# The second stage of a graph network: from generators with due times to a planner of operations for all engines

## The chip, the cores and the metric

The kernel runs on one core of one Trainium2 chip. The metric is the device time of one execution in microseconds (us). A core has a matrix engine (TensorE, PE in the profile), a vector engine (VectorE, DVE), an activation engine (ScalarE, ACT), a small general engine (GpSimd, POOL), and a queue engine (SyncE, SP) from which most transfers (DMAs) are issued. Each runs its own list of instructions in the order in which the program holds them, and waits on semaphores for the others. All data are float32.

## The reference, cut to what matters

`x` is 128 graphs of 64 nodes with 256 features: 8192 rows. Each layer is `x = layernorm(x + f(x))`.

```python
# layer 0: A = adj * adj            h = relu(A (x W1)); h = relu(A (h W2)); f = A (h W3)
# layer 1: U = eigenvectors of a normalised Laplacian of adj
#          f = U (relu((U.T x) W1 + b1) W2 + b2)
# layer 2: h = relu(adj (x Wg0 + bg0)); h = relu(adj (h Wg1 + bg1))
#          for p in 1..4: an LSTM over windows of p nodes; its last state
#          overwrites node p-1 of every window; f = h
# layer 3: h = x W + b_lin; s = (h h.T) * adj, zeros to -1e16; f = softmax(s) h + b
```

## The kernel before

The 8192 rows stand in the on-chip memory as one tile `X` of 64 tiles of 128 rows (a tile holds two graphs). Four tiles make a group, so there are 16 groups.

**Stage one** is layer 0 of all groups, with the eigenvector computation of layer 1 threaded between its matmuls on the DVE. It ends about 860 us into the run and isn't touched by the change, but for the order in which it takes the groups and where their rows lie.

**Stage two** is layers 1 to 3, group by group. A group is a Python generator (`group`, calling `layer1`, `layer2`, `lstm`, `layer3`) that issues instructions and yields the time at which it can go on. Up to `WAYS = 3` groups are open. The PE's order is written by hand: `now` is a clock that advances by an account of each matmul, and at each turn the loop at the end takes, of the groups whose yielded time has come, the oldest one (or, when no group is left to open, the one that is least far on). The yielded times are coarse constants, for example:

```python
MOVE, MIXED, LIN, CONV, NORM, SOFT = 1.2, 1.2, 1.5, 1.8, 5.2, 5.2
CELL = {256: 3.8, 168: 2.2, 128: 1.9}
...
ready.append(now[0] + NORM + more + (0.8 if ready else 0.0))
```

DVE, ACT and POOL aren't ordered by hand in stage two: a scheduler of the framework orders what was issued, with two copies put ahead (`high_priority`). Scratch tiles come from rotating pools: `pw` with 5 buffers, `pv` with 4, `pg` with 3 each for gates, cell and state, and `psb`, the 8 banks of PSUM.

The chains that cross engines, by their lines in the profile:

- layer 1 (`layer1`): `ps<-u,X`, copy to `w`, `ps<-bw,w`, add of the bias on DVE (L971), relu on ACT (L725), `ps<-ut,v`, copy (L979), `ps<-bw,v`, add to `X` (L986), and the norm: `bn_stats` and `bn_aggr` (L551, L552) on DVE, two operations on POOL (L553, L554), and `X<-X,ln_mv,ln_rs` (L564) on DVE. Layer 2 then begins with `ps<-adT,X`.
- LSTM step: per half `h` and gate four matmuls (two with `wih` on the inputs, two with `whh` on the state `hs`; each shows as two records), then `tanh` on ACT (L1030), the cell update on DVE (L1034, L1036, L1038), `tanh` of the cell (L1039), and the new `hs` (L1041), which the `whh` matmuls of the next step read. The last state of a window is written back into `hT`, a tile `w` (L1051).
- layer 3: transposes of `X` (L926), two copies (L1120, L1124), `ps<-w,dw`, identity with bias (L1130), scores (L1146), softmax on DVE and ACT (L1150 to L1159), transposes of `att`, copy `eT` (L1166), `ps<-w,v`, add to `X` (L1176), norm, output.

The last two groups (`ENDING`) take layer 3 in two halves of two tiles and do the last step of the norm on ACT (L562).

Of the kernel before, what the change touches and what calls it, by code (L numbers as in the profile page):

```python
# [1 line left out]

# [8 lines left out]
F32 = mybir.dt.float32  # L11
# [4 lines left out]
N = 64  # L16
# [24 lines left out]
class Timed:  # L41
# [6 lines left out]
    def __getattr__(self, name):  # L48
        def give(out, *args, **kw):
            self.free[0] = max(self.free[0], self.until[0]) + self.least + 0.0009 * max(0, np.prod(out.shape[1:]) - 64)  # L50
            return getattr(self.engine, name)(out, *args, **kw)  # L51

        return give

# [484 lines left out]
LEAD = 10  # L539
# [57 lines left out]
def kernel(  # L597
# [51 lines left out]
    X = keep.tile([P, NT, D], F32, name="X")  # L649
# [4 lines left out]
    nc.scalar.dma_start(X[:, 2:4, :], x_t[:, 2:4, :])  # L654
    for t in range(2):
        nc.sync.dma_start(X[:, t, :], x_t[:, t, :])
# [6 lines left out]
    for t in range(4, NT, 2):  # L663
        nc.sync.dma_start(X[:, t:t + 2, :], x_t[:, t:t + 2, :])
# [79 lines left out]
    def layer0(g):  # L744
        xs = X[:, 4 * g:4 * g + 4, :]
# [108 lines left out]
        for t in (2, 0):  # L854
            p = tl(psa, [P, 2, D], "ps", bufs=6)
            mm(p, sqT2, s3[:, t:t + 2, :])
            yield now[0]
            x2 = xs[:, t:t + 2, :]
            VL.tensor_add(x2, p, x2)
            norms.extend(scalar_norm(tc, small, x2, half, spare))  # L860

# [45 lines left out]
    pg = ctx.enter_context(tc.tile_pool(name="pg", bufs=WAYS, reuse_waits="tile"))  # L907
    pw = ctx.enter_context(tc.tile_pool(name="pw", bufs=5, reuse_waits="tile"))
    pv = ctx.enter_context(tc.tile_pool(name="pv", bufs=4, reuse_waits="tile"))
    psb = ctx.enter_context(tc.tile_pool(name="psb", bufs=8, space=bass.MemoryType.PSUM, reuse_waits="tile"))  # L910
# [10 lines left out]
    now[0] = due[0] = 0.0  # L921
    MOVE, MIXED, LIN, CONV, NORM, SOFT = 1.2, 1.2, 1.5, 1.8, 5.2, 5.2
    CELL = {256: 3.8, 168: 2.2, 128: 1.9}

    def turn(out, in_):
        PE.transpose(out, in_, ident)  # L926
        now[0] += 0.11

    def work():
        return tl(pw, [P, 1024], "w")  # L930

    def work2():
        return tl(pv, [P, 512], "v")

    spare[0] = lambda: work2()[:, :D]

    def ps4(shape=(P, 512)):
        return tl(psb, list(shape), "ps")
# [4 lines left out]
    def mixed(src, rhs, ready):  # L943
# [3 lines left out]
        for t in range(4):  # L947
            if t % 2 == 0:
                yield ready[t // 2]
            for c in range(2):  # L950
                mm(ps[c][:, t * P:(t + 1) * P], src[:, t, c * P:(c + 1) * P], rhs)
        with tc.high_priority(offset=1500):
            V.tensor_copy(dst[:, 0, :], ps[0])
        S.copy(dst[:, 1, :], ps[1])
        yield now[0] + MIXED
        return dst

    def norm(xs, t, ready, more=0.0, scalar=False):
        rows_norm(tc, small, xs[:, t:t + 2, :], half, scalar)
        ready.append(now[0] + NORM + more + (0.8 if ready else 0.0))  # L960

    def layer1(xs, ready):
        a = yield from mixed(xs, u2, ready)
        for t in range(0, 4, 2):
            V.tensor_add(xs[:, t:t + 2, :], xs[:, t:t + 2, :], ub2.unsqueeze(1).to_broadcast([P, 2, D]))
        h = as3(work2(), 4)
        for t in range(0, 4, 2):
# [5 lines left out]
            yield now[0]  # L973
        yield now[0] + LIN
        z = work2()
        p = ps4((P, 4, P))
        for t in range(4):
            mm(p[:, t, :], h[:, t, :], ut2)
        S.copy(as3(z, 4), p)  # L979
        yield now[0] + MOVE  # L980
        ready = []
        for t in range(0, 4, 2):
            p = ps4((P, 2, D))
            for j in range(2):
                mm(p[:, j, :], z[:, (t + j) * P:(t + j + 1) * P], bw2)
            V.tensor_add(xs[:, t:t + 2, :], p, xs[:, t:t + 2, :])  # L986
            norm(xs, t, ready, 2.0)
            yield now[0]
        return ready

    def lstm(hT, p, first, nw):
# [6 lines left out]
        for t in range(p):  # L998
# [4 lines left out]
            G = tl(pg, [P, 2048], "gates")[:, :2 * len(names) * n].rearrange("p (q h n) -> p q h n", h=2, n=n)  # L1003
            gate = {q: G[:, i] for i, q in enumerate(names)}
            units = [(h, q) for h in range(2) for q in names]

            ahead = {}
            early = units[:2] if t else []
            for h, q in early:
                m = slice(("ifgo".index(q) * 2 + h) * P, ("ifgo".index(q) * 2 + h + 1) * P)  # L1010
                ahead[h, q] = pp = ps4()[:, :n]
                for k in range(2):
                    mm(pp, wi[:, k, m], xt[k], k == 0, False)
            if t:
                yield ready
            if p > 1 and not t:
                c = tl(pg, [P, 512], "c")[:, :2 * n].rearrange("p (h n) -> p h n", h=2)
            new = None if last else tl(pg, [P, 512], "hs")[:, :2 * n].rearrange("p (h n) -> p h n", h=2)
            for h, q in units:
                j = 2 * "ifgo".index(q) + h  # L1020
                m = slice(j * P, (j + 1) * P)
                pp = ahead.get((h, q))
                if pp is None:
                    pp = ps4()[:, :n]
                    for k in range(2):
                        mm(pp, wi[:, k, m], xt[k], k == 0, k == 1 and not t)
                if t:
                    for k in range(2):
                        mm(pp, wh[:, k, m], hs[:, k, :], False, k == 1)
                S.activation(gate[q][:, h, :], pp, AF.Tanh, bias=bias[:, j:j + 1], scale=0.5 if q == "g" else 0.25)  # L1030
                if q == "g":
                    to = gate["g"][:, h, :] if t or p == 1 else c[:, h, :]
                    if t:
                        V.scalar_tensor_tensor(c[:, h, :], gate["f"][:, h, :], 1.0, c[:, h, :], op0=ALU.add,  # L1034
                                               op1=ALU.mult)
                    V.scalar_tensor_tensor(to, gate["i"][:, h, :], 1.0, gate["g"][:, h, :], op0=ALU.add, op1=ALU.mult)  # L1036
                    if t:
                        V.scalar_tensor_tensor(c[:, h, :], c[:, h, :], 0.5, to, op0=ALU.mult, op1=ALU.add)  # L1038
                    S.activation(gate["i"][:, h, :], c[:, h, :] if p > 1 else to, AF.Tanh, scale=0.5)  # L1039
                if q == "o" and not last:  # L1040
                    V.scalar_tensor_tensor(new[:, h, :], gate["o"][:, h, :], 1.0, gate["i"][:, h, :], op0=ALU.add,  # L1041
                                           op1=ALU.mult)
                if q == "o":
                    if h == 0:
                        yield now[0]
                elif h == 1 or len(units) == 8:
                    yield now[0]
# [7 lines left out]
            ready = now[0] + CELL[n]  # L1055
            hs = new
        return ready

    def layer2(xs, g, ready):
        a = yield from mixed(xs, adT2, ready)  # L1060
        g1 = as3(work(), 4)
        ready = []
        for t in range(0, 4, 2):
            p = ps4((P, 2, D))
            for j in range(2):
                run(p[:, j, :], [(a[:, k, (t + j) * P:(t + j + 1) * P], cw0[:, k, :]) for k in range(2)])
            V.tensor_add(g1[:, t:t + 2, :], p, wide["c_b0"].unsqueeze(1).to_broadcast([P, 2, D]))
            relu(g1[:, t:t + 2, :], g1[:, t:t + 2, :])
            ready.append(now[0] + CONV)
            yield now[0]  # L1070
        a = yield from mixed(g1, adT2, ready)
        hT = tl(pw, [P, 1024], "w").rearrange("p (k n b) -> p k n b", k=2, b=8)
        for c in range(2):
            p = ps4((P, 4, P))
            run(p, [(cw1[:, k, c * P:(c + 1) * P], a[:, k, :]) for k in range(2)])
            h = work2()
            V.scalar_tensor_tensor(as3(h, 4), rs_row.unsqueeze(1).to_broadcast([P, 4, P]), cb1[:, c:c + 1], p,
                                   op0=ALU.mult, op1=ALU.add)
            S.activation(hT[:, c, :, :].rearrange("p n b -> p b n"), as3(h, 8), AF.Relu, scale=2.0)
            yield now[0]  # L1080
        ready = now[0] + CONV
        for p, first, nw in ((1, 0, 32), (1, 32, 32), (2, 0, 32), (3, 0, 21), (4, 0, 16)):
            if first == 0:
                yield ready
            ready = yield from lstm(hT, p, first, nw)
        hb = as3(work(), 2)
        V.tensor_copy(as3(hb[:, 0, :], 8), hT[:, 0, :, :].rearrange("p n b -> p b n"))
        S.copy(as3(hb[:, 1, :], 8), hT[:, 1, :, :].rearrange("p n b -> p b n"))
        yield ready + 1.6
        ready = []  # L1090
        for t in range(0, 4, 2):
            p = ps4((P, 2, D))
# [169 lines left out]
```

## Time and profile before

| | |
|---|---|
| time, three runs | 2534.43, 2536.52, 2536.97 us; median 2536.52 |
| span of the profiled execution | 2539.1 us |
| PE busy | 2494.8 us (98%) |
| weight loads busy | 2196.2 us (86%) |
| DVE, ACT, POOL busy | 1407.8, 1090.6, 134.2 us |
| mean granted PE clock | 0.993 |
| DMA | 32.09 MB, mean 13 GB/s |

The PE is busy nearly throughout, so the chain of waits that ended last is 91% PE. A busy PE isn't a PE at its peak, since matmuls are pipelined and their ends are modelled. What a change of order can move is therefore in the rest: the idle time of the PE by place, the stretches in which its granted clock is below 1, and the distance between the starts of its matmuls. A window of the trace gives, for a stretch of time, how long each engine was busy in it, with the number of its instructions, the granted clock, the share of the DMA engines and their rate.

### The profile page before, as it was taken

Reading aid. Unit: us, or ns where it says so; the run is one execution under the profiler, and the core shown is the slowest. Engines: PE = TensorE matmul, PEld = TensorE weight load, DVE = VectorE, ACT = ScalarE, POOL = GpSimd, SP = SyncE. Lnnn points to the kernel's source line nnn. Section 1 sums busy time; section 2 is a strip of 40 time slices with the busy share of each in tenths; the row PEclk is TensorE's granted clock in tenths of the full one; section 3 lists DMA queues with packets and bytes.
Section 4 is the critical chain, followed back from the end, with each engine's and each line's share of the span. In section 5 each row is a group of like instructions: output and inputs, shape, how many; then the busy total and the mean of one; then the engine's idle time right before and its main releaser. Section 6 shows DMA issues by size and latency. Waiting matters only on the chain.

```text
span 2539.1 us, 39015 instructions
## 1 busy us (share of the span) xinstructions
PE 2494.8 (98%) x15020; PEld 2196.2 (86%) x15020; DVE 1407.8 (55%) x4996; ACT 1090.6 (43%) x2706; POOL 134.2 (5%) x316
## 2 busy tenths in 40 slices
PE   9999999999999999999999999999999999999997
PEld 7788887888878889998989889898998998978996
DVE  6888777778885433454453543544445345353235
ACT  2344333433333344445344444444444534535454
POOL 0000000000000100000000000000000000010001
PEclk9999999999999999999999999999999999999998
DMA  6000000000000300000000000000000000000000
GB/s 219 1 1 1 1 1 1 1 1 1 1 1 1 117 1 1 10 9 1 9 9 1 9 1 10 9 1 9 1 9 9 1 9 9 1 9 1 1 1 26
DMA packets 24634, 32.09 MB, mean 13 GB/s; under 512 B 2176, under 2 KB 21376, under 8 KB 24448
## 3 DMA queue, kind: packets, MB, share of 16 engines
q1 hardware_dynamic: 24096, 29.32, 3.4%
q8 instruction: 118, 1.93, 0.3%
q14 instruction: 68, 0.56, 0.1%
q10 hardware_dynamic: 352, 0.28, 0.0%
HBM read 21.20 MB, written 8.39 MB: 12 GB/s over the span
## 4 chain that ended last, share of the span: by engine, by line
PE 91%; DVE 5%; POOL 2%; issue 1%; DMA 0%; ACT 0%; SPq 0%; ACTq 0%; POOLq 0%; DVEq 0%
PE ps L716 88%; PE ps L926 2%; POOL ln_rs L554 1%; DVE X L564 1%; DVE ln_st L551 1%; DVE D L51 1%; PE ps L1146 1%; PE pc L93 1%; DMA X<-in_x_dram 0%; POOL ln_rs L553 0%; DVE tw L51 0%; DVE ln_mv L552 0%; DVE X L1176 0%; DVE X L986 0%; DVE X L1096 0%
## 5 line engine op out<-in xcount | busy, mean ns | idle before, releaser
L716 PE MATMUL ps<-w,wih 128*128 128x256 f32 (+2 forms) x4992 | 894.0, 319 | 1.8 <-DVE w L1051 1.8
L716 PEld LDWEIGHTS ps<-w,wih 128*128 128x128 f32 x4992 | 760.9, 191 | 47.8 <-issue 5.7
L1030 ACT ACTIVATE gates<-ps,cbi 128x128 f32<-128x128 f32 (+2 forms) x1248 | 499.3, 410 | 523.3 <-PE ps L716 516.2
L716 PE MATMUL ps<-hs,whh 128*128 128x128 f32 (+2 forms) x3072 | 540.5, 303 | 6.2 <-DVE hs L1041 6.2
L716 PEld LDWEIGHTS ps<-hs,whh 128*128 128x128 f32 x3072 | 453.9, 191 | 32.9 <-issue 11.2
L1036 DVE SCALAR_TENSOR_TENSOR gates<-gates 128x256 f32<-128x256 f32 (+2 forms) x256 | 89.3, 349 | 297.4 <-ACT gates L1030 297.4
L716 PE MATMUL ps<-aw,h 128*128 128x256 f32 x1024 | 227.2, 379 | 0.0
L716 PEld LDWEIGHTS ps<-aw,h 128*128 128x128 f32 x1024 | 192.9, 190 | 25.9 <-ACT h L725 0.5
L725 ACT ACTIVATE h<-h 128x512 f32<-128x512 f32 x128 | 80.5, 629 | 170.0 <-DVE h L51 169.8
L1039 ACT ACTIVATE gates<-c 128x128 f32<-128x128 f32 (+2 forms) x288 | 98.1, 341 | 114.1 <-DVE c L1038 87.9
L1034 DVE SCALAR_TENSOR_TENSOR c<-gates,c 128x128 f32<-128x128 f32 (+2 forms) x192 | 62.6, 326 | 139.4 <-ACT gates L1030 138.2
L1051 DVE SCALAR_TENSOR_TENSOR w<-gates 128x256 f32<-128x256 f32 (+2 forms) x160 | 59.6, 376 | 108.5 <-PE ps L716 73.5
L716 PE MATMUL ps<-ss,tw 128*128 128x256 f32 x512 | 117.9, 380 | 0.0
L716 PE MATMUL ps<-ss,aw 128*128 128x256 f32 x512 | 117.3, 379 | 0.0
L716 PE MATMUL ps<-m,aw 128*128 128x256 f32 x512 | 117.1, 380 | 0.0
L716 PE MATMUL ps<-aw,m 128*128 128x512 f32 x256 | 114.8, 594 | 0.0
L1041 DVE SCALAR_TENSOR_TENSOR hs<-gates 128x128 f32<-128x128 f32 (+2 forms) x192 | 62.6, 326 | 93.6 <-ACT gates L1039 52.4
L553 POOL TENSOR_SCALAR ln_rs<-ln_mv 128x2 f32<-128x2 f32 x96 | 26.2, 273 | 1558.4 <-DVE ln_mv L552 1557.9
L716 PEld LDWEIGHTS ps<-ss,aw 128*128 128x128 f32 x512 | 96.6, 190 | 12.8
L716 PEld LDWEIGHTS ps<-ss,tw 128*128 128x128 f32 x512 | 96.3, 190 | 12.9 <-issue 0.2
L564 DVE TENSOR_SCALAR X<-X,ln_mv,ln_rs 128x256 f32<-128x256 f32 x176 | 64.7, 410 | 75.9 <-POOL ln_rs L554 75.9
L716 PEld LDWEIGHTS ps<-m,aw 128*128 128x128 f32 x512 | 95.6, 190 | 12.6 <-issue 0.5
(294 smaller groups left out, 3107.4 us busy)
## 6 DMA issues: line engine op xcount, KB each, us to landing
X<-in_x_dram SPq DMA_DIRECT2D x30, 256.0 KB, 6.3
out_dram<-X SPq DMA_DIRECT2D x28, 256.0 KB, 2.1
wih<-in_c_ih_dram SPq DMA_DIRECT2D x4, 1024.0 KB, 7.2
aw<-in_a_w_dram SPq DMA_DIRECT2D x3, 1024.0 KB, 10.3
whh<-in_c_hh_dram SPq DMA_DIRECT2D x3, 1024.0 KB, 9.4
out_dram<-X SPq DMA_DIRECT2D x8, 128.0 KB, 1.7
aw<-in_a_w_dram SPq DMA_DIRECT2D x1, 512.0 KB, 5.8
cw<-in_c_w_dram SPq DMA_DIRECT2D x2, 256.0 KB, 5.1
```

What stands on the lines that cost most here:

```text
L51: return getattr(self.engine, name)(out, *args, **kw)
L553: nc.gpsimd.tensor_scalar(rs, mv[:, :, 1], EPS, None, op0=ALU.add)
L564: nc.vector.tensor_scalar(x[:, t, :], x[:, t, :], mv[:, t, 0:1], rs[:, t:t + 1], op0=ALU.subtract, op1=ALU.mult)
L716: PE.matmul(out, lhsT, rhs, start=start, stop=stop)
L725: S.activation(dst, src, AF.Relu)
L926: PE.transpose(out, in_, ident)
L1030: S.activation(gate[q][:, h, :], pp, AF.Tanh, bias=bias[:, j:j + 1], scale=0.5 if q == "g" else 0.25)
L1034: V.scalar_tensor_tensor(c[:, h, :], gate["f"][:, h, :], 1.0, c[:, h, :], op0=ALU.add, op1=ALU.mult)
L1036: V.scalar_tensor_tensor(to, gate["i"][:, h, :], 1.0, gate["g"][:, h, :], op0=ALU.add, op1=ALU.mult)
L1039: S.activation(gate["i"][:, h, :], c[:, h, :] if p > 1 else to, AF.Tanh, scale=0.5)
L1041: V.scalar_tensor_tensor(new[:, h, :], gate["o"][:, h, :], 1.0, gate["i"][:, h, :], op0=ALU.add, op1=ALU.mult)
L1051: V.scalar_tensor_tensor(hT[:, h, slice(first + p - 1, first + nw * p, p), :], gate["o"][:, h, :].rearrange("p (w b) -> p w b", b=8), 1.0, ...
```

## The change

Stage two isn't issued by generators any more. Each operation is first *noted*: engine, instruction, cost, and the parts of tiles that it reads and writes. `Part` stands for a view of a tile, `Op` for a noted operation, `Noted` for an engine that only notes, and `Plan` keeps the account. Dependences come out of overlaps of the parts. Then `Plan.run` goes through time: at each turn every engine has a list of operations whose inputs are there by the account, and the one that can start first is issued; among those of an engine that can start within 0.02 us of its first, the oldest group's comes first, and on the PE, once no group is left to open, that of the group with most operations left. A scratch tile gets its place (one of 8 PSUM banks, 5 `w`, 4 `v`, 3 of each of the LSTM's) only when its first operation is issued, namely that which comes free first. The orders of PE, DVE, ACT and POOL are then all held as issued.

```diff
+    LAG = {"PE": 0.20, "DVE": 0.118, "ACT": 0.137, "POOL": 0.04, "SP": 2.0}
...
+        def rank(op):
+            if op.engine == "PE" and not todo:
+                return -going[op.group]
+            return op.group or 99
...
+                for op in ops:
+                    t = max(self.free[e], op.ready)
+                    for tile in op.tiles:
+                        if tile.real is None and tile.slot is None:
+                            t = max(t, min(self.slots[tile.tag]))
+                    if t < 1e9:
+                        first.append((t, op))
+                if first:
+                    t0 = min(t for t, _ in first)
+                    t, op = min((x for x in first if x[0] <= t0 + 0.02), key=lambda x: (rank(x[1]), x[1].rank))
+                    if best is None or t < best[0]:
+                        best = t, op
...
+            if cost is None and self.engine == "DVE":
+                cost = {"bn_aggr": 0.082, "reciprocal": 0.095}.get(name, 0.067 + n / 960)
...
+            elif cost is None and self.engine == "ACT":
+                cost = (0.145 if bank else 0.110) + n * 0.00083
```

The memory of the rows changes too. `X` holds 44 tiles, not 64. Stage one takes groups 11 to 15 first, then 0 to 10; when one of the first five is through, its rows go to HBM (`rest`) and rows of groups 0 to 4 are loaded in their place. In stage two the rows of group `g + 11` come back when group `g` (0 to 4) has been put out. The room that this frees is for a variant (`PAIRS`) that is switched off here.

```diff
-    X = keep.tile([P, NT, D], F32, name="X")
+    X = keep.tile([P, NT - 4 * LATE, D], F32, name="X")
...
+        def change():
+            nc.sync.dma_start(rest[g], xs)
+            for t in (0, 2):
+                nc.sync.dma_start(xs[:, t:t + 2, :], given(order[g + LATE])[:, t:t + 2, :])
...
+        if g < LATE:
+            Q.dma_start(xs, rest[g])
...
+    with tc.manual_schedule(engines={mybir.EngineType.PE, mybir.EngineType.DVE, mybir.EngineType.Activation,
+                                     mybir.EngineType.Pool}):
+        plan.run([left_over] + [lambda g=g: group(g) for g in range(NT // 4)], WAYS)
```

Small edits go with it: the copies `hb` ahead of layer 2's last transposes are cut in two (each 128x256 rather than 128x512), the output leaves in transfers of 128 KB only, layer 3's transposes for `hn` are noted after its scores, and the norms that stage one leaves over are noted as the lowest in rank.

## The prediction

> **What bounds the kernel now.** I read the windows first, cut so that each stretch with idle time of the PE (second column: busy us) stands alone.
>
> ```profile
> 0.00:860.00 860.00, 854.38 (x4058) 699.14 (x4059) 655.82 (x2854) 318.02 (x781) 35.07 (x102) 1.00 0.06 20
> 860.00:900.00 40.00, 35.87 (x227) 31.72 (x226) 25.84 (x66) 15.06 (x38) 7.70 (x18) 0.91 0.33 131
> 1180.00:1240.00 60.00, 57.53 (x362) 50.69 (x361) 32.21 (x92) 25.98 (x62) 6.04 (x12) 1.00 0.03 10
> 1430.00:1450.00 20.00, 17.63 (x126) 17.00 (x125) 12.32 (x39) 6.73 (x19) 3.91 (x7) 1.00 0.08 27
> 1450.00:1634.00 184.00, 184.00 (x1238) 167.14 (x1237) 80.74 (x226) 86.41 (x215) 7.59 (x16) 1.00 0.01 4
> 1634.00:1656.00 22.00, 19.64 (x136) 18.82 (x136) 13.91 (x45) 7.24 (x20) 4.36 (x8) 1.00 0.07 25
> 2250.00:2275.00 25.00, 19.25 (x106) 17.83 (x106) 14.30 (x41) 5.55 (x13) 4.11 (x8) 0.80 0.06 22
> 2275.00:2490.00 215.00, 214.16 (x1475) 200.21 (x1474) 77.22 (x225) 106.27 (x270) 3.68 (x8) 1.00 0.00 1
> 2490.00:2531.50 41.50, 33.09 (x221) 27.04 (x219) 25.84 (x93) 19.70 (x51) 10.00 (x28) 0.84 0.08 26
> 2531.50:2539.10 7.60, 0.00 (x0) 0.00 (x0) 1.82 (x7) 2.18 (x4) 2.61 (x8) 0.50 0.21 70
> ```
>
> Between stalls the PE is never idle, with DVE and ACT under half busy (80.74 and 86.41 of 184 us). The reader is to see that all that an order can save lies in a few places. Idle in stage two: 4.1 us at its start; 2.5 and 2.4 at 1180 and 1430, and the 2.4 comes back at 1634, 1840 and 2044, once in two groups: 12 us; 5.8 at 2250, where the last group enters; 0.8 before 2490; 8.4 in the last 41.5; and 7.6 after the last matmul. The clock (seventh figure) adds to this: cut to its half-speed stretches,
>
> ```profile
> 890.00:897.00 7.00, 5.93 (x25) 5.62 (x26) 2.56 (x6) 1.80 (x3) 0.92 (x2) 0.52 0.00 1
> 2259.00:2269.20 10.20, 6.43 (x27) 6.14 (x28) 5.14 (x14) 1.87 (x4) 1.55 (x3) 0.50 0.01 2
> 2511.60:2518.40 6.80, 5.85 (x19) 5.02 (x20) 3.59 (x15) 3.63 (x10) 1.95 (x7) 0.50 0.13 41
> 2525.20:2539.10 13.90, 5.19 (x12) 3.00 (x12) 4.61 (x17) 3.54 (x8) 2.61 (x8) 0.50 0.12 38
> ```
>
> half of the PE's busy time is lost in each: 3.0 + 3.2 + 2.9 + 2.6 us. So **42.7 us** are in reach: start 7.1, middle 11.9, entry of the last group 9.8 (with the 0.8), end 13.9. The 7.6 us after the last matmul are a chain of its own.
>
> The PE's waits, and the timeline of the stall that comes back, say what ends them:
>
> ```profile
> PE ps L716 <- DVE X L564: 6.9, 5, 2.8
> PE ps L716 <- DVE hs L1041: 6.2, 5, 1.3
> PE ps L716 <- ACT v L725: 4.4, 3, 3.0
> ```
>
> ```profile
> 1429.37 1.89 PE L716 MATMUL ps<-bw,v 128*128 128x256 f32 x8
> 1432.88 4.73 PE L716 MATMUL ps<-w,wih 128*128 128x168 f32 x32
> 1434.26 0.68 DVE L986 TENSOR_TENSOR X<-ps,X 128x512 f32<-128x512 f32 x1
> 1437.33 0.70 POOL L554 TENSOR_TENSOR ln_rs<-ln_rs,half 128x2 f32<-128x2 f32 x1
> 1438.07 0.73 DVE L564 TENSOR_SCALAR X<-X,ln_mv,ln_rs 128x256 f32<-128x256 f32 x2 [0.57 <-POOL ln_rs L554]
> 1438.63 1.13 PE L716 MATMUL ps<-adT,X 128*128 128x128 f32 x8 [1.03 <-DVE X L564]
> 1442.28 0.98 PE L716 MATMUL ps<-hs,whh 128*128 128x168 f32 x5 [1.34 <-DVE hs L1041]
> ```
>
> The 32 records take 4.73 us together, so the distance of two starts is about 0.143 us, and my counts of PE work use that distance. The matmuls `bw,v` that feed L986 of the first half start at 1429.37 and are over within a microsecond, but L986 runs only at 1434.26, since the DVE works off another group's adds, norm and LSTM first; its norm then ends at 1438.8. Two stalls of 1.0 and 1.3 us follow.
>
> **What the Trainium skill says.** "TensorE: Matmul & The Clock Gate", Part 1 (The HAM clock gate): an idle activity window of about 3.4 us drops the PE to half clock, and a busy one is needed to get it back. The trace agrees in kind: half-clock stretches of 6.8 and 10.2 us, each behind a cluster of waits. The same page, Architectural detail: ACT and DVE take their instructions strictly first in, first out, which is the stall shown above. "Trainium Kernel Development and Optimization", Performance Expectations: matmul busy time is a poor measure because matmuls are pipelined; here a 168-column record has a mean duration of 307 ns at a distance of 143.
>
> **The change part by part.**
>
> *PE work.* The built order has the same number of PE instructions as before, form by form, and the same order in stage one. Waits that are already met cost nothing now: between stalls the PE loses nothing, though a third of its instructions wait for something. 0 us.
>
> *Orders of DVE and ACT.* What counts is the PE work that stands between the last matmul of a chain and the first that reads its result, against the chain's length. I counted it in both built orders by start distances.
> - Reader `adT,X` behind `bw,v`, in the middle: 7.2 us of work before, too little with the queue shown; 8.9 at least after, and the DVE no longer serves first what isn't due. The stall should go.
> - Reader `whh,hs` behind the last `o` gate: at least 2.8 us before, 1.55 after. The chain: 0.20 from the end of a gate's matmuls (1432.88 + 8 x 0.143 = 1434.02) to its start on ACT (1434.22 in the timeline), L1030 0.365, 0.397 or 0.472 (128, 168, 256 columns), L1041 0.291, 0.331 or 0.423, and 0.09 for two hand-overs: 0.95, 1.02, 1.19. It fits, with 0.5 us to spare where 2 were.
> - Reader `ident,att` behind the scores: 5.2 us before, 3.5 after. The chain of five DVE operations and two Exp (0.411 each) is about 2.9. It fits.
>
> I then went through the whole order after with such durations, instruction by instruction, each engine in its order, and noted where a reader comes too early. **Start of stage two** (7.1 before): one place of 0.3, no cluster, so no half clock; I take 1.0. **Middle** (11.9): 1.35 where the second group's `w` is read by `wih`, 0.8 and 0.4 where new groups start, and about zero in each later pair of groups; I take 3.5. **Entry of the last group** (9.8): nothing; I take 0.5. **End** (13.9): the three last groups run side by side, so nearly all readers find work ahead. Two are left: 0.7 for `eT`, and the last matmuls, whose `hn` add (0.685) stands on the DVE behind the previous half's two L1176 (0.465), two `bn_stats` (0.408) and two `bn_aggr` (0.166): 0.93 + 0.82 + 0.33 + 0.69 and hand-overs of 0.3, less some overlap: 2.9. With half a clock behind it I take 6.0. **Sum 11.0 of 42.7: 31.7 us less.**
>
> *After the last matmul.* L1176, norm, POOL's four, ACT's two, a transfer: the same instructions, 7.6 us. 0.
>
> *Rows through HBM.* Ten transfers of 512 KB, 5.2 MB beside 32.09. 1 MB lands in 7 to 10 us now. In stage one five groups (5 x 860 / 16 = 270 us) lie between leaving and use; in stage two group g + 11 enters some eight groups (8 x 104 us) after group g is out. They queue on SP, whose other work is outputs that nobody waits for. 0.
>
> *Small edits.* 32 copies more on DVE and ACT in all, at most 0.15 us each over 1670 us of half-idle engines; 28 more issues on SP. Hidden. The left-over norms are of group 10, needed 900 us later. 0.
>
> Prediction: 2536.5 - 31.7 = **2505 us**.
>
> **Rivals.**
> 1. *Thin margins.* Chains have 0.5 us to spare, not 2. If DVE or ACT is late by more than that at two places in each group's twelve LSTM steps, by 0.4 us: 15 x 2 x 0.4 = 12 us come back: 2517. For it: every engine is held in a strict order, so one late instruction delays all behind it. Against it: the account's durations (0.334 for a 128x256 DVE operation plus 0.118 of lag) match the rows (0.419), and DVE and ACT are under half busy.
> 2. *Only the ends gain* or only the middle, because a queue I take as free isn't: half of 31.7 remains to be had: 2521. For it: each of the two parts rests on a few DVE queues of some twelve operations. Against it: both were walked through with the same durations.
> 3. *Slower or the same.* With fixed orders an error in POOL's or a transfer's time lets all engines wait once per group: over 2.0 us in each of 16 groups eats the 31.7: 2537 and more. For it: GpSimd spans are rough. Against it: each norm's chain has 8.9 us of PE work over it in the middle, and a norm takes about 4 (from 1434.26, L986, to 1438.07 with the wait).
>
> **How the numbers follow.** 0.74 for my forecast, 0.12 for the first rival, 0.08 for the second, 0.06 for the third. The low end takes only the 3.6 us of the two late places at the end as left: 2536.5 - 39 = 2497. The high end lies between the first rival and the second: 2519. A gain under 0.2% (5 us) lies only in the third rival: 0.02; slower 0.04.
>
> **What would show it.** Right: the stall of 1.0 + 1.3 us once in two groups is gone, PE idle between 900 and 2490 is under 5 us in all, clock 1.00 up to the last 20 us, and 2490 on shows one late `hn` add. Wrong: many waits of PE on `hs` L-lines of 0.1 to 0.5 us (first rival); PE idle around the start or the last group's entry as before (second); waits on DMA rows, or on POOL through `X`, in each group (third). A changed distance between matmul starts would break the base of all of it.

## The result, and the profile after

The changed kernel takes **2553.45 us** (median of 4 runs, 2552.30 to 2554.64); the kernel before, run beside it, takes 2535.52 (4 runs, 2534.43 to 2536.97). The ratio is **1.0070, 95% interval 1.0053 to 1.0088**: slower by 0.7%, where a gain of 31.7 us was forecast. The two traces differ by less than the medians do (spans of 2539.1 and 2550.5 us): the execution of before that was profiled took 2540.9 us, more than any of these four, at a mean granted clock of 0.993 where most others of this kernel show 0.996. The prediction's ledger was read from that execution, so part of its half-clock loss is missing from most others.

Two windows of the kernel before that the prediction has only in pieces, then the windows of the kernel after. The columns are length, busy us and instructions of PE, PEld, DVE, ACT and POOL, clock, DMA share, GB/s.

```profile
900.00:2250.00 1350.00, 1338.07 (x8942) 1220.28 (x8941) 606.94 (x1713) 623.79 (x1551) 71.07 (x144) 1.00 0.02 6
2250.00:2490.00 240.00, 233.41 (x1578) 218.04 (x1578) 91.53 (x266) 111.81 (x282) 7.79 (x16) 0.98 0.01 3
```

```profile
860.00:900.00 40.00, 39.58 (x254) 34.95 (x253) 25.43 (x58) 23.96 (x55) 6.53 (x14) 1.00 0.33 131
900.00:2250.00 1350.00, 1324.41 (x8816) 1191.29 (x8815) 621.57 (x1735) 615.06 (x1522) 71.99 (x153) 1.00 0.02 8
2250.00:2490.00 240.00, 239.82 (x1573) 224.32 (x1573) 82.47 (x231) 116.46 (x298) 3.52 (x8) 1.00 0.01 3
2490.00:2580.00 90.00, 42.07 (x326) 33.40 (x324) 43.26 (x137) 28.55 (x70) 14.91 (x40) 0.92 0.05 18
```

Read against the ledger of the prediction: the start of stage two (first row) and the entry of the last group (third) are cured, as forecast; idle time of the PE is 0.4 and 0.2 us there. The middle, 11.9 us idle before, now has 1350 - 1324.41 = **25.6 us**, though the clock is 1.00 throughout. The waits of the PE in that window (total us, times, longest):

```profile
PE ps L151 <- ACT w L151: 7.3, 16, 1.3
PE ps L151 <- DVE X L151: 5.9, 14, 1.2
PE ps L151 <- ACT att L151: 4.7, 13, 0.4
PE ps L151 <- ACT v L151: 4.2, 5, 0.8
PE ps L151 <- DVE w L151: 2.4, 2, 2.2
PE ps L151 <- ACT gates L151: 0.8, 4, 0.2
```

All operations of stage two are issued from one helper line (L151), so the tile's name has to tell which reader it is. `hs`, the wait that I feared most, is not in the list at all. `att`, the softmax, comes 13 times in 13 groups and never over 0.4 us: a wait that is built into each group. `X` comes 14 times, and its reader is now `ident,X`, the transposes of layer 3's input behind layer 2's norm; `adT,X`, which waited before, doesn't wait in this window any more.

Even 25.6 us is too little. The modelled end of a matmul lies 0.16 us or so behind the start of the next, so a wait shorter than that disappears in "busy". So I also summed, over both traces, the distance from each matmul record's start to the next, less the usual (median) distance behind records of its shape. Time lost in this way, called *lost by starts* below: before 50.0 us in all, of which 10.3 between 900 and 2250; after **60.9 in all, of which 38.9** there. What is taken as one shape moves such a sum by 1 to 3 us. The difference of 10.9 is close to that of the two spans (11.4). The middle loses 28.6 us more, and start and entry give 16.5 back.

One group's softmax in the middle, in the timeline of after (start, us, engine, operation, tiles, count, and in brackets the idle time before it):

```profile
1507.21 1.20 PE L151 MATMUL ps<-w 128*64 128x64 f32 x32
1508.34 1.09 PE L151 MATMUL ps<-ident,w 128*128 128x128 f32 x8
1508.45 0.42 DVE L151 TENSOR_TENSOR v<-ps,adst 128x256 f32<-128x256 f32 x1 [5.36 <-PE ps L151]
1508.91 0.29 DVE L151 TENSOR_SCALAR v<-v 128x256 f32<-128x256 f32 x1
1509.24 0.43 DVE L151 TENSOR_TENSOR v<-v 128x256 f32<-128x256 f32 x1
1509.27 1.89 PE L151 MATMUL ps<-w,wih 128*128 128x256 f32 x8
1509.70 0.42 DVE L151 TENSOR_REDUCE mx<-v 128x4 f32<-128x256 f32 x1
1510.15 0.43 DVE L151 TENSOR_TENSOR v<-v,mx 128x256 f32<-128x256 f32 x1
1510.61 0.84 ACT L151 ACTIVATE att<-v 64x256 f32<-64x256 f32 x2 [2.82 <-DVE v L151]
1511.50 0.66 PE L151 MATMUL ps<-ident,att 128*128 128x128 f32 x4 [0.34 <-ACT att L151]
1512.00 1.03 PE L151 MATMUL ps<-w,wih 128*128 128x256 f32 x4
...
1513.25 0.57 ACT L151 COPY v<-ps 128x512 f32<-128x512 f32 x1
...
1513.87 1.99 PE L151 MATMUL ps<-w,v 128*128 128x256 f32 x8 [0.84 <-ACT v L151]
```

Two things in it contradict the account by which `Plan.run` made the order.

*Transposes.* Eight of them (`ident,w`) take the PE from 1508.34 to 1509.27: 0.116 us each; four (`ident,att`) from 1511.50 to 1512.00. The account's `turns` prices each at 0.218. A group has 28 (8 each for `hb`, `X` and `hn`, 4 for `att`): 28 x 0.109 = **3.05 us of PE work per group that the plan has and the chip doesn't**.

*Dependent operations of one engine.* The account (the planner's table of costs) lets an operation start when the one before it on its engine has cost its 0.334 us, dependent or not. Here each reads the result of the last, and the distances behind the 128x256 ones are 0.46, 0.46, 0.45 and 0.46 us, and 0.33 behind the `TENSOR_SCALAR` that the account prices at 0.200: about 0.125 us more each. From the first to the Exp the account has 4 x 0.334 + 0.200 + 0.118 = 1.65 us, the trace 2.16.

Call the PE work that stands between the last matmul of a chain and the first that reads its result the reader's *cover*. Between the end of the scores and `ident,att` the plan sees 8 x 0.218 + 8 x 0.215 = 3.5 us of PE work (0.215 is the usual distance of a 256-column record). There are 2.65 on the chip, under a chain of 3.16: 0.51 us lost, of which 0.34 shows as idle. The next loss follows by the queue: `v`'s copy stands on ACT behind the gates of another group, and `w,v` comes 1.0 us late.

The Trainium skill's "Perfetto Trace Analysis", section Optimizing Scalar/DVE Operations, says that the recorded latency of a DVE instruction holds a write-acknowledgement half that overlaps with the next instruction. The trace agrees: rows of 0.42 to 0.43 us, of which the account counts 0.334. That a dependent operation has to wait this half out would fit the distance measured; the page doesn't say it, and no run here separates it from other reasons.

### The profile page after: what moved, and what is told of

Its sections match the earlier page's. It is cut to its first block, busy times and chain, and to the rows that moved or that the text cites. A ratio compares the mean times of both kernels' runs of the same rounds, so it can differ in the third digit from the quotient of the medians.

```text
span 2550.5 us, 39082 instructions
## 1 busy us (share of the span) xinstructions
PE 2500.0 (98%) x15020; PEld 2182.9 (86%) x15020; DVE 1428.3 (56%) x5012; ACT 1099.2 (43%) x2722; POOL 137.0 (5%) x316
## 4 chain that ended last, share of the span: by engine, by line
PE 87%; DVE 10%; ACT 1%; issue 1%; DMA 0%; POOL 0%; SPq 0%; ACTq 0%; POOLq 0%; DVEq 0%
PE ps L151 56%; PE ps L915 30%; DVE X L151 2%; DVE st L151 2%; DVE v L151 1%; DVE w L151 1%; DVE D L52 1%; ACT w L151 1%; DVE mv L151 1%; PE pc L276 1%; DMA X<-in_x_dram 0%; POOL rs L151 0%; DVE tw L52 0%; DVE sm L151 0%; ACT gates L151 0%
## 5 line engine op out<-in xcount | busy, mean ns | idle before, releaser
L151 PE MATMUL ps<-w,wih 128*128 128x256 f32 (+2 forms) x4992 | 895.1, 319 | 7.2 <-ACT w L151 4.2
L151 PEld LDWEIGHTS ps<-w,wih 128*128 128x128 f32 x4992 | 764.0, 191 | 58.4 <-ACT w L151 8.9
L151 ACT ACTIVATE gates<-ps,cbi 128x256 f32<-128x256 f32 (+2 forms) x1248 | 505.2, 409 | 511.2 <-PE ps L151 497.0
L151 PE MATMUL ps<-hs,whh 128*128 128x128 f32 (+2 forms) x3072 | 539.3, 303 | 0.0
L151 PEld LDWEIGHTS ps<-hs,whh 128*128 128x128 f32 x3072 | 453.4, 191 | 14.9 <-issue 0.5
L151 DVE SCALAR_TENSOR_TENSOR gates<-gates 128x256 f32<-128x256 f32 (+2 forms) x256 | 89.5, 350 | 356.0 <-ACT gates L151 355.9
L151 DVE SCALAR_TENSOR_TENSOR c<-gates,c 128x128 f32<-128x128 f32 (+2 forms) x192 | 62.8, 327 | 201.9 <-ACT gates L151 201.6
L151 ACT ACTIVATE gates<-c 128x128 f32<-128x128 f32 (+2 forms) x288 | 98.3, 342 | 149.6 <-DVE c L151 148.7
L151 DVE SCALAR_TENSOR_TENSOR hs<-gates 128x128 f32<-128x128 f32 (+2 forms) x192 | 62.6, 328 | 104.1 <-ACT gates L151 100.8
L151 POOL TENSOR_SCALAR rs<-mv 128x2 f32<-128x2 f32 x96 | 22.3, 232 | 1593.1 <-DVE mv L151 1593.0
L915 PEld LDWEIGHTS ps<-ss,aw 128*128 128x128 f32 x512 | 96.6, 190 | 12.8
L915 PEld LDWEIGHTS ps<-aw,m 128*128 128x128 f32 x256 | 47.8, 190 | 49.3 <-issue 46.2
L1056 ACT COPY s<-ps 128x512 f32<-128x512 f32 x32 | 18.8, 586 | 145.2 <-PE ps L915 145.2
```

The source lines that it names most:

```text
L151: getattr(e, name)(*[real(x) for x in args], **{k: real(v) for k, v in kw.items()})
L915: PE.matmul(out, lhsT, rhs, start=start, stop=stop)
L1056: S.copy(s3[:, t:t + 2, :], p)
```

## The experiments

Theory A: the two wrong constants make the loss, and the planner is sound. Its rivals: the account needs more reserve for each hand-over (B); the strict orders of DVE, ACT and POOL are themselves the harm, or the rows through HBM are (C).

**One constant each, both, and reserve instead.** The first changes the price of a transpose alone.

```diff
-        plan.note("PE", [("transpose", (out, in_, ident), {}) for out, in_ in pairs], 0.218 * len(pairs))
+        plan.note("PE", [("transpose", (out, in_, ident), {}) for out, in_ in pairs], 0.109 * len(pairs))
```

> Only the account's price of a transpose changes, from 0.218 to 0.109 us, which is what four transposes of one operation take in the trace of the change (0.437 us for 4). Theory A (the account is wrong in two constants: transposes at twice their time, and no latency between two DVE operations that depend on each other, 0.125 us each): about half of the 39 us that the PE waits or loses between 900 and 2250 us goes, some 20 are left; time about 2533, near the kernel before. Theory B (chains are planned without a reserve and every small delay costs): the PE comes sooner to each reader, so waits stay at 39 or grow; time 2553 or more. Theory C (rows through HBM, or the strict orders as such): no change, 2553.

The second adds a delay between dependent operations of one engine, and nothing else. The 0.125 us for DVE is measured; the 0.1 for ACT is a guess.

```diff
+    SELF = {"PE": 0.0, "DVE": 0.125, "ACT": 0.1, "POOL": 0.0, "SP": 0.0}
...
-                other.ready = max(other.ready, t + op.cost if other.engine == e else end)
+                other.ready = max(other.ready, t + op.cost + self.SELF[e] if other.engine == e else end)
```

> Only the account's latency between dependent operations on one engine is added (DVE 0.125 us, ACT 0.1 us); transposes stay at twice their time. Theory A: about half of the waits in the middle goes, as in the run with transposes alone, some 20 us left, time about 2533. Theory B: a little reserve where there was none, so a gain of the same kind, 2530 to 2550. Theory C: 2553.

The third has both diffs.

> Both constants are set right. Theory A: about 11 us of waits left between 900 and 2250 and about 5 us in the last 60 us, time 2505 to 2515, faster than the kernel before by 1% (2535.5). Theory B: at best as the better of the two alone, about 2535. Theory C: 2553.

The fourth leaves both errors in and gives 0.3 us more to every hand-over of DVE and ACT.

```diff
-    LAG = {"PE": 0.20, "DVE": 0.118, "ACT": 0.137, "POOL": 0.04, "SP": 2.0}
+    LAG = {"PE": 0.20, "DVE": 0.418, "ACT": 0.437, "POOL": 0.04, "SP": 2.0}
```

> The account of the change, with its two errors, and 0.3 us more of lag behind each DVE and ACT operation. Theory A: the PE's time runs ahead of the account by 3 us in each group whatever the lag, so the waits stay near 38 us between 900 and 2250; time 2545 to 2555. Theory B: the reserve takes up the delays, waits in the middle fall below 10 us, time 2510 to 2525. Theory C: 2553.

Measured beside the kernel before at 2538.62 us. The last three columns are of the middle, 900 to 2250 us: the PE's idle time, the time lost by starts, and the cover of `ident,att` in its 13 groups.

| kernel | us | ratio to before | 95% interval | idle | by starts | cover |
|---|---|---|---|---|---|---|
| transposes | 2529.71 | 0.9965 | 0.9952 to 0.9978 | 11.2 | 17.5 | 3.1 to 3.5 |
| dependence | 2525.30 | 0.9950 | 0.9933 to 0.9966 | 11.7 | 16.8 | 3.5 |
| both | 2517.29 | 0.9916 | 0.9901 to 0.9930 | 8.1 | 11.0 | 4.4 to 5.2 |
| reserve | 2553.56 | 1.0057 | 1.0042 to 1.0072 | 23.9 | 39.8 | 2.65 |
| (after) | | 1.0070 | 1.0053 to 1.0088 | 25.6 | 38.9 | 2.6 |
| (before) | | | | 11.9 | 10.3 | 5.2 to 5.8 |

The middle's window with the transposes mended:

```profile
900.00:2250.00 1350.00, 1338.83 (x8948) 1212.91 (x8946) 636.53 (x1777) 623.87 (x1545) 77.53 (x160) 1.00 0.02 8
```

with the dependence mended, then its waits:

```profile
900.00:2250.00 1350.00, 1338.34 (x8952) 1212.84 (x8951) 627.74 (x1776) 631.83 (x1546) 76.22 (x160) 1.00 0.02 8
```

```profile
PE ps L152 <- ACT w L152: 6.0, 13, 0.6
PE ps L152 <- ACT att L152: 5.7, 13, 0.5
```

and with both, again with the waits:

```profile
900.00:2250.00 1350.00, 1341.95 (x8980) 1219.79 (x8979) 624.30 (x1778) 630.69 (x1548) 78.75 (x160) 1.00 0.02 8
```

```profile
PE ps L152 <- ACT w L152: 3.2, 7, 0.8
PE ps L152 <- DVE w L152: 3.0, 5, 1.1
PE ps L152 <- ACT v L152: 0.9, 2, 0.7
PE ps L152 <- DVE X L152: 0.7, 2, 0.3
```

and with the reserve, with the first of its waits:

```profile
900.00:2250.00 1350.00, 1326.09 (x8810) 1194.67 (x8809) 619.54 (x1724) 620.60 (x1528) 73.94 (x150) 1.00 0.02 8
```

```profile
PE ps L151 <- DVE X L151: 13.0, 18, 1.3
PE ps L151 <- ACT att L151: 4.7, 13, 0.4
```

A holds for the two constants: either one turns the loss into a gain, and together the PE's idle time in the middle is 8.1 us, against 25.6. The transposes are the sharper proof, since B forecast 2553 or more for them. That the second delay works as a right price, and not as a reserve put inside the chains, isn't separated: no run overprices it. The waits tell the two errors apart: with the transposes still wrong, `att` keeps a wait in each of 13 groups and `w` has 13 too, and the cover of `att` has the eight transposes in it; with both right, `att` has none, and `w` waits for ACT 7 times. Pricing the dependence has a side effect: in the trace of that kernel the DVE runs other groups' operations in the gaps of the softmax, and in the group at 1495 us the chain from scores to `ident,att` takes 4.1 us, not 3.16. The gains don't add up: against the kernel after at its own ratio they are about 1.1, 1.2 and 1.5% of the time. Either mended constant removes part of the same waits. The single constants gained more than the 2533 that I gave each, and both together, at 2517.3, came out above the 2505 to 2515; beside the before of the first comparison their ratio would give 0.9916 x 2535.5 = 2514, so that miss is small.

Right prices don't make the planner better than the old order in the middle: by starts it loses 11.0 us there, the kernel before 10.3. The gain of "both" is made at the start of stage two, at the entry of the last group, and in the last 50 us.

The reserve falls as tried, but it never reached the softmax: the cover of `ident,att` is 2.65 us in all 13 groups, no more than in the kernel after. The account's own constants give a reason (an estimate). Without the reserve the chain needs 0.20 + 1.65 + 2 x 0.32 + 0.14 = 2.6 us, with it 3.2, since two hand-overs lie in it. Both stay under the 3.5 us of cover that the plan believes it has, so it adds no work. Where the reserve did act it shifted waits: those of `w` on ACT (7.3 us) are gone, those on `X` grew from 5.9 to 13.0. A larger reserve wasn't tried.

What fell short lies at the end. With both constants right the last matmuls start at 2502.4 us, but 12.8 us follow them (8.35 in the kernel after). The timeline of that kernel:

```profile
2499.91 2.86 PE L152 MATMUL ps<-w,v 128*128 128x256 f32 x12 [0.29 <-ACT v L152]
...
2501.08 0.48 DVE L152 SCALAR_TENSOR_TENSOR X<-ps,sm,X 128x256 f32<-128x256 f32 x1 [0.60 <-PE ps L152]
...
2507.29 0.86 DVE L152 SCALAR_TENSOR_TENSOR X<-ps,sm,X 128x256 f32<-128x256 f32 x2
2508.08 0.74 DVE L152 BATCH_NORM_STATS2 st<-X 128x6 f32<-128x256 f32 x2
...
2511.35 1.09 ACT L152 ACTIVATE X<-X,nm,rs 128x256 f32<-128x256 f32 x2 [0.57 <-POOL nm L152]
```

Twelve matmul records of several halves leave at once, and DVE works off their adds and norms from 2501.1 to 2509 without a pause; POOL, ACT and the transfer fill the rest. There the DVE has become the bound.

**Rows kept in place.** Groups 11 to 15 no longer leave for HBM; in exchange a pool of small tiles has 2 buffers for 4.

```diff
-LATE = 5
+LATE = 0
...
-    small = ctx.enter_context(tc.tile_pool(name="small", bufs=4))
+    small = ctx.enter_context(tc.tile_pool(name="small", bufs=2))
...
-    for g in order[1:LATE] + order[2 * LATE:]:
+    for g in order[1:]:
```

> The change without the way of the rows through HBM: X holds all 64 tiles again, stage one takes the groups in their order (two small buffers fewer in stage one make the room). Theory A: 2553 +- 3, as the change, since the rows cost nothing. Theory C, rows: faster than the change by 5 us or more.

Measured 2552.76 us, ratio 1.0062 (1.0047 to 1.0077), with before at 2536.56. The ratio lies within the interval of the kernel after, and the middle loses 38.7 us by starts, as there. The rows cost nothing that shows, as forecast.

**Only the PE's order held.** DVE, ACT and POOL are no longer bound to the plan's order.

```diff
-    with tc.manual_schedule(engines={mybir.EngineType.PE, mybir.EngineType.DVE, mybir.EngineType.Activation,
-                                     mybir.EngineType.Pool}):
+    with tc.manual_schedule(engines={mybir.EngineType.PE}):
```

> The planner's order is held on the PE alone; DVE, ACT and POOL are ordered by the framework's scheduler, as in the kernel before. Theory A: the PE's order is the same just-in-time order, and now the other engines don't follow the account either, so more waits: 50 us in the middle in place of 39, time 2560 to 2580. Theory C, strict orders on four engines cost as such: faster than the change, 2535 to 2545.

Measured 2577.96 us, 1.0159 (1.0142 to 1.0176). Its waits in the middle begin with

```profile
PE ps L151 <- ACT att L151: 27.1, 12, 2.8
PE ps L151 <- DVE X L151: 7.7, 14, 1.4
```

The time lies in A's range, and the middle loses 55.0 us by starts, where 50 were expected. The softmax now holds the PE for 2.3 us on average in each of 12 groups: the cover is 2.65 us as in the kernel after, but the DVE puts operations of other groups into the chain, and in the group at 1522.9 us the first Exp starts 3.85 us after the chain's first DVE operation (2.16 in the kernel after). Under this PE order the strict orders aren't the harm; even made by a wrong account they are worth 1%. Whether they cost something under right prices wasn't tried.

**The wrong price in the kernel before.** Its generators kept an account too, with 0.11 for a transpose (`turn`). Here it gets the planner's price.

```diff
     def turn(out, in_):
         PE.transpose(out, in_, ident)
-        now[0] += 0.11
+        now[0] += 0.218
```

> The kernel before, with the price of a transpose in its own account doubled to 0.218 us, as in the change. Theory A: the coarse due times hold work back long enough to take the error up, so the time stays within 0.4% of the kernel before (2530 to 2540), and it is the just-in-time order that makes the change sensitive to it. If a wrong price costs by itself, whatever the order: slower by 10 us or more.

Measured 2532.57 us, 0.9983 (0.9976 to 0.9990): within the bound given for it, and if anything faster. The middle, and the window in which the last group enters:

```profile
900.00:2250.00 1350.00, 1335.88 (x8958) 1219.21 (x8957) 613.41 (x1739) 619.50 (x1545) 75.50 (x152) 1.00 0.02 6
2250.00:2490.00 240.00, 238.21 (x1613) 221.94 (x1612) 90.11 (x266) 117.93 (x299) 8.36 (x20) 1.00 0.01 3
```

The 6.6 us of idle time at the entry before are 1.8, in what is merely another order. The middle has 14.1 us of idle time in place of 11.9: its stalls on `X` and `hs` come 6 times each, not 4. So the same error that costs the planner some 25 us (1.0070 against 0.9965) costs the older account about 2 in the middle and nothing in all. That its coarse due times leave margins that hold the error is my reading; no trace shows the due times.

**More prices, and edits for the end.** Both constants, two more prices from the trace (1.13 us for the 32 scores matmuls, planned at 0.92; 0.43 for an Exp of 64x256, planned at 0.32), and two edits for the end: among the last groups an older one leads the next by 20 operations on the PE, and group 13 also takes layer 3 in halves, with its norm's last step on ACT.

```diff
-                return -going[op.group]
+                return -going[op.group] + 20 * op.group
...
-ENDING = (14, 15)
+ENDING = (13, 14, 15)
...
-        plan.note("PE", calls, 0.23 * nt)
+        plan.note("PE", calls, 0.28 * nt)
...
-            S.activation(e[hs, :, hs], s[hs, :, :], AF.Exp)
+            S.activation(e[hs, :, hs], s[hs, :, :], AF.Exp, cost=0.11 + 0.00125 * nt * N)
```

> Both constants right, the price of the scores (0.28 for 0.23 us a tile) and of Exp (0.43 for 0.32 us) from the trace too, and two edits for the end: the last three groups take layer 3 in halves, not two, and an older group leads the next by 20 operations when no group is left to open. Theory A: middle as with both constants or 2 us better, the end 5 us better: 2508 to 2514. If what is left comes from the end's DVE work alone, no gain from the prices and 2512.

Measured **2512.43 us, 0.9903 (0.9889 to 0.9918)**, within what was expected. The last matmuls start at 2502.3 and 7.9 us follow. Its windows:

```profile
900.00:2250.00 1350.00, 1341.73 (x8990) 1220.65 (x8989) 626.63 (x1780) 629.77 (x1548) 77.75 (x160) 1.00 0.02 8
...
2490.00:2600.00 110.00, 8.88 (x70) 6.06 (x68) 13.18 (x49) 9.06 (x21) 6.96 (x20) 0.96 0.04 14
```

By the medians this is 5 us less than "both"; by the ratios, each beside its own before, it is 3 us, and their intervals overlap. Which part brings it? One kernel has the two prices without the edits for the end, the next those edits without the prices.

> The tuned kernel without its two edits for the end: transposes, dependence, scores and Exp priced by the trace. If the prices of scores and Exp matter: 2 us less than with both constants alone, 2515. If the end is what is left: 2517 +- 2.

> Both constants right and the two edits for the end, with scores and Exp priced as in the change. If the end is what is left: 2512 +- 2, as tuned. If the prices bring the gain: 2517.

Measured, with before at 2537.09: 2520.50 (0.9933, 0.9915 to 0.9951) and 2518.34 (0.9925, 0.9909 to 0.9940). Neither part alone brings anything over "both", and the first missed what was expected of it; the second came near the 2517 that stood for a gain by the prices, which the first denies. The traces settle part of it. By starts the middle loses 9.2 us with all edits and 9.3 with the two prices alone, but 11.0 with "both" and with the edits for the end alone: the prices are worth under 2 us there. The rest lies in the last fifty microseconds. The last matmuls start at 2502.3 with all edits, at 2510.9 with the prices alone, at 2507.7 with the edits for the end alone, and 7.9, 8.0 and 9.0 us follow. Which edit makes the end better stays open, since each shuffles that order.

## Why the prediction was wrong

The same places, in idle time of the PE plus half-clock loss as the prediction counts them, in us:

| place | before | predicted | after |
|---|---|---|---|
| start of stage two | 7.1 | 1.0 | 0.4 |
| middle (by starts) | 11.9 (10.3) | 3.5 | 25.6 (38.9) |
| entry of the last group | 9.8 | 0.5 | 0.2 |
| end, up to the last matmul | 13.9 | 6.0 | 11.7 |
| after it | 7.6 | 7.6 | 7.7 |

*Right:* start and entry, the tail, and the rows through HBM. That the small edits cost nothing wasn't tried by itself. The stall of `adT,X` behind L986 that came back once in two groups is gone, and `hs` waits nowhere in the middle. The entry is no proof of the reasoning: the old kernel with its wrong price lost most of that stall too, by another order alone.

*The step that failed* is the walk through the order after: "I then went through the whole order after with such durations", with its "Middle: I take 3.5". The walk repeats the account's own two errors, as its numbers show. Its PE work took a transpose at the time of a whole matmul of the same width, which is two records: "5.2 us before, 3.5 after" for `ident,att` is 2.65 on the chip, short by 8 x 0.109 us. Its chains took DVE operations at their distance when nothing depends on anything: "about 2.9" is 3.16 here. So 3.5 of cover over a chain of 2.9 became 2.65 under 3.16, and the middle, forecast at 3.5 us, had 25.6. A plan and a walk through it that share their constants agree: the walk found almost no waits because the planner had left none by the same numbers. The 3.5 was too low beyond that: with both constants right, in another order, the middle still has 8.1 us. The trace of before had the right price, in the timeline of its PE:

```profile
1497.26 1.04 PE L926 MATMUL ps<-ident,w 128*128 128x128 f32 x8
1498.14 6.21 PE L716 MATMUL ps<-w,wih 128*128 128x256 f32 x28
```

Eight in 0.88 us, 0.11 each, the very number in `turn`. The diff doubled it, and I passed over it.

*The first rival* had the kind of loss (thin margins, short waits in each group) and looked in the wrong place: its sign, waits on `hs`, isn't there. The argument against it was wrong: "the account's durations match the rows". A 128x256 row of 0.42 us does match 0.334 + 0.118 for a reader on another engine; for a reader on the same engine it doesn't. It was also mis-sized, at 12 us: 38.9 were lost, 3.0 per group. *The third rival*'s sign, waits through `X` in each group, did come (14 times, 5.9 us), at `ident,X`, not at `adT,X`, over which the prediction had counted 8.9 us of work. With the dependence priced, no matmul of the middle waits on `X`, while POOL's prices stayed as they were; so removing them took no change in POOL's prices.

*The end* was the right kind at half its size. The late `hn` add came:

```profile
2534.63 1.13 PE L151 MATMUL ps<-w,v 128*128 128x256 f32 x4 [0.57 <-ACT v L151]
...
2537.57 0.88 DVE L151 SCALAR_TENSOR_TENSOR X<-ps,sm,X 128x256 f32<-128x256 f32 x2
...
2538.70 0.72 DVE L151 TENSOR_SCALAR X<-X,mv,rs 128x256 f32<-128x256 f32 x2
...
2539.95 0.66 DVE L151 TENSOR_TENSOR w<-ps,wide_d_b 128x512 f32<-128x512 f32 x1
2540.75 2.04 PE L151 MATMUL ps<-w,v 128*128 128x256 f32 x4 [4.99 <-DVE w L151]
```

The last matmuls wait 5.0 us for the `hn` add at 2539.95, not 2.9: beside the operations that I listed, other halves' norms, sums and adds stand before it on the DVE.

What isn't settled: why the middle keeps 8 us of waits with both constants right, and whether the second constant is a price or a reserve in the right place.

## What to carry to other kernels

An order made just in time is as good as its account: before trusting one, lay its planned starts beside the traced starts, kind by kind, and price a dependent operation apart from an independent one. Work out the PE's cover for a chain from distances of starts in the trace of the kernel before, not from the planner's constants, or the walk inherits the plan's errors. 0.3 us of reserve for each hand-over did not stand in for right prices here; at the softmax it added no work at all. And compare place by place: with right prices the planner won at the start, the entry and the end, not in the middle.

## What the runs showed of the hardware that was not expected

An fp32 transpose of 128x128 through the PE takes 0.109 us from start to start and leaves one record, while its time is half of an fp32 matmul of 128 columns (two records, 0.223 us). The Trainium skill's "TensorE: Matmul & The Clock Gate", Part 4 (PE-mode transpose), gives about 275 ns for one of bf16 in a kernel's context. The records here agree, with a median of 273 ns in `ident,att`; but what the PE pays in a run of them is the distance, and that is 0.4 of it.

Dependent DVE operations start about 0.12 us later than independent ones at each of three widths (medians of start distances in SBUF, from the LSTM's and the softmax's operations): 0.326 against 0.20 to 0.21 us at 128 columns, 0.368 against 0.25 at 168, 0.46 against 0.33 to 0.34 at 256.

In these traces the clock goes by how busy the PE was in a fixed window, not by one long wait. In all twelve traces the changes of the granted clock lie whole multiples of 3.413 us apart. I cut the traces along that grid and counted each matmul record, those of transposes too, as busy for its usual distance. The clock fell to half in 28 places, each behind a window in which the PE was busy for at most 0.37 of the time. Of the other 8743 windows at full clock (from 20 us on) none was under 0.41. Transposes count as work for the clock: four of the windows at 0.41 to 0.45 have 0.26 to 0.34 of it in transposes, and no drop followed. Several short waits are enough: in the kernel with the reserve the window before 1716.29 has 0.35 with no wait over 1.5 us, and a half-clock stretch of 3.41 us follows.

```profile
1712.88:1716.29 3.41, 1.70 (x13) 1.15 (x11) 3.31 (x11) 0.61 (x2) 1.83 (x4) 1.00 0.00 0
1716.29:1719.70 3.41, 3.26 (x10) 2.77 (x11) 1.78 (x5) 1.51 (x4) 0.00 (x0) 0.50 0.00 0
```

The middle of the kernel after, with one wait of 2.2 us and many short ones, keeps 1.00, since its least busy window there has 0.50; the window before the drop at 2538.7, inside the wait of 5.0 us, has 0.09. The Trainium skill's "TensorE: Matmul & The Clock Gate", Part 1, puts the drop behind an idle window of some 3.4 us. The length agrees with these traces; a window didn't have to be idle here.
